# A layernorm stage in a macaron block: the first two token tiles one by one, and later statistics put behind earlier normalisations

## The chip, the cores and the metric

One Trainium2 chip, one of its cores. The metric is the device time of one execution in microseconds (us). A kernel is run several times; the median is what counts. One further execution is recorded by the hardware profiler: its profile gives every instruction's start and duration on the five engines (TensorE "PE", VectorE "DVE", ScalarE "ACT", GpSimd "POOL", SyncE "SP") and the transfers.

## The reference

The input x has 8 x 256 tokens of 256 float32 values. The block adds three terms to it:

```python
x = x + 0.5 * ffn(layernorm(x))
x = x + attention(layernorm(x))          # top-32 keys chosen by an indexer
x = x + 0.5 * ffn(layernorm(x))

def layernorm(x): return (x - mean(x)) / sqrt(var(x) + 1e-5)

def ffn(x):                               # 8 experts of width 176, 2 per token, and a shared one of 352
    scores = softmax(x @ gate_w); topk_w, topk_idx = top_k(scores, 2)
    routed = sum over the chosen experts of weight * (silu(x @ w_gate[e]) * (x @ w_up[e])) @ w_down[e]
    shared = silu(x @ sw_gate) * (x @ sw_up) @ sw_down
    return routed + shared
```

The change concerns the first line only: the layernorm ahead of the first FFN.

## The kernel before, in words

The 2,048 tokens are 16 tiles (NT) of 128 tokens, one token per partition. x stays in SBUF for the whole kernel. The kernel is written as dataflow on tiles; a scheduler at build time orders each engine's instructions and sets the waits, and that order is then fixed in the program. Each engine runs its own list strictly in order. `tc.issue_after(ins)` adds an edge that only tells this scheduler to put what is traced inside it behind `ins` on the same engine. A tile pool gives a tag a number of buffers (`bufs`): the next tile of that tag waits until the readers of the one that had its buffer are done, and a DMA that reads it is done when it has landed.

The first stage, up to the routing of the first FFN, runs like this:

- **Loads.** SP issues the loads of x by groups of tiles (L101 to L104), then sw_up (wsu_sb, L107) and sw_down (wsd_sb, L109 and L115). ScalarE's queue issues sw_gate with gate_w (wsg_sb, L105 and L106). x's groups are tiles 0-1, 2-3, 4-7, 8-11, 12-15. The transfers issued from SP and ScalarE share eight completion counters in turn, and a transfer on a counter that is in use waits on its issuing engine until the earlier one has landed.
- **Layernorm by group** (`layernorm`, L220). For each tile of the group VectorE takes statistics (bn_stats into st, L226; bn_aggr into mv, L227), then for the whole group adds epsilon (ve, L229). In the first FFN (`table=True`) ScalarE takes a square root (sd, L236) and VectorE the reciprocal (rstd, L237). In front of the square root of a group that starts at tile g0, L234 asks the scheduler to stay behind the copy of tile g0 - 3. Then for each tile VectorE writes xn = (x - mean) * rstd (L259), SP writes xn to xn_dram in HBM (L263), from where the routed experts gather tokens later, TensorE transposes its two halves into PSUM (pt, L266) and ScalarE copies them into xnT (L267). xn has five buffers (L258), pt two.
- **Expert loads.** After each group's layernorm the loop at L468 issues the next two of six expert loads on SP (L470): gate and up of the first half of the inputs, gate and up of the second, and the two halves of w_down (128-partition loads for gate and up, 88 partitions for w_down; 704 KB each). With five groups the first three issue a pair each.
- **Gate projection.** For each tile TensorE multiplies xnT with wsg_sb (pg, L476; a float32 product counts as two instructions in the profile for each of the two halves, so four a tile), ScalarE copies the eight router logits (lg, L483) and takes the Silu (sg, L485). pg has two buffers. The square root and the Silu use different activation tables, so ScalarE reloads a table whenever it changes from one to the other.
- **Shared expert, ahead of time.** The scheduler fills in the first tiles' second product with wsu_sb (pu, L493) and its product with sg (gt, L501); their transposes (ptg, L512) come behind the last pg.
- **Route.** When all 16 tiles' logits are there VectorE picks the two experts of each token (top, L291, and what follows), and the routed experts run block by block.

The second FFN and the attention use the same `layernorm` with `table=False`; the second FFN uses the same list `groups`.

Of the kernel before, what the change touches and what calls it, by code (L numbers as in the profile page):

```python
# [23 lines left out]
def macaron_kernel(  # L24
# [19 lines left out]
    nc = tc.nc  # L44

    B, S, D = x_in.shape
    NT = B * S // P
# [38 lines left out]
    x = res.tile([P, NT, D], F32, name="x")  # L86
# [11 lines left out]
    wk_sb = wts.tile([P, KD, HD], F32, name="wk_sb")  # L98
    wv_sb = wts.tile([P, KD, HD + HI], F32, name="wv_sb")

    starts = [0, 2, 4, 8, 12, NT]  # L101
    groups = [range(a, b) for a, b in zip(starts, starts[1:])]
    for g in groups:
        nc.sync.dma_start(out=x[:, g.start : g.stop, :], in_=xr[:, g.start : g.stop, :])  # L104
    nc.scalar.dma_start(out=wsg_sb[:, :, 0:HS], in_=sw_gate.rearrange("(k p) h -> p k h", p=P))  # L105
    nc.scalar.dma_start(out=wsg_sb[:, :, HS:], in_=gate_w.rearrange("(k p) e -> p k e", p=P))  # L106
# [108 lines left out]
    contents.append(lambda: nc.gpsimd.memset(inner, 1.0))  # L215
    contents.append(lambda: nc.gpsimd.memset(inner[:, :, 0:1], 0.0))

    turned_x = {}

    def layernorm(tiles, xn_dram=None, table=False):  # L220

        g0, n = tiles[0], len(tiles)
        mv = small.tile([P, n, 2], F32, tag="mv", name=f"mv_{g0}")
        for j, i in enumerate(tiles):
            st = small.tile([P, 6], F32, tag="st", name=f"st_{i}")
            nc.vector.bn_stats(st, x[:, i, :])  # L226
            nc.vector.bn_aggr(mv[:, j, :], st)  # L227
        ve = small.tile([P, n], F32, tag="ve", name=f"ve_{g0}")
        nc.vector.tensor_scalar(ve, mv[:, :, 1], EPS, None, ALU.add)  # L229
        rstd = small.tile([P, n], F32, tag="rstd", name=f"rstd_{g0}")  # L230
        if table:
            sd = small.tile([P, n], F32, tag="sd", name=f"sd_{g0}")
            with ExitStack() as order:
                if g0 - 3 in turned_x:  # L234
                    order.enter_context(tc.issue_after(turned_x[g0 - 3].ins))
                nc.scalar.activation(sd, ve, AF.Sqrt)  # L236
            nc.vector.reciprocal(rstd, sd)  # L237
        else:


            half = small.tile([P, n], I32, tag="half", name=f"half_{g0}")
            nc.vector.tensor_scalar(half, ve.bitcast(I32), 1, None, ALU.arith_shift_right)
            guess = small.tile([P, n], I32, tag="guess", name=f"guess_{g0}")
            nc.vector.tensor_tensor(
                guess, magic.to_broadcast([P, n]), half, ALU.subtract
            )
            y = guess.bitcast(F32)
            for it in range(3):
                sq = small.tile([P, n], F32, tag="sq", name=f"sq_{g0}_{it}")
                nc.vector.tensor_tensor(sq, y, y, ALU.mult)  # L250
                nc.vector.scalar_tensor_tensor(sq, sq, -0.5, ve, ALU.mult, ALU.mult)
                z = rstd
                if it < 2:
                    z = small.tile([P, n], F32, tag="z", name=f"z_{g0}_{it}")
                nc.vector.scalar_tensor_tensor(z, sq, 1.5, y, ALU.add, ALU.mult)
                y = z
        for j, i in enumerate(tiles):
            xn = small.tile([P, D], F32, tag="xn", name=f"xn_{i}", bufs=5)  # L258
            nc.vector.tensor_scalar(  # L259
                xn, x[:, i, :], mv[:, j, 0:1], rstd[:, j : j + 1], ALU.subtract, ALU.mult  # L260
            )
            if xn_dram is not None:
                nc.sync.dma_start(out=xn_dram[i * P : (i + 1) * P, 0:D], in_=xn)  # L263
            pt = psum.tile([P, KD, P], F32, tag="C", name=f"pt_{i}")
            for k in range(KD):
                nc.tensor.transpose(pt[:, k, :], xn[:, k * P : (k + 1) * P], ident)  # L266
            turned_x[i] = nc.scalar.copy(xnT[:, :, i * P : (i + 1) * P], pt)  # L267

    def route(n, lg, xn_dram, place, block, pool, keep, meanwhile, last):

# [179 lines left out]
    def ffn(n, pool, block_pool, behind):  # L450
# [14 lines left out]
        block = counted(f"block_{n}", [[1, NB], [0, NT * K]], dtype=BF16, pool=tables)  # L465
        while contents:
            contents.pop(0)()
        for tiles in groups:  # L468
            layernorm(tiles, xn_dram, table=(n == 0))
            for load in expert_loads[0:2]:  # L470
                load()
            del expert_loads[0:2]
            for i in tiles:
                pg = psum.tile([P, HS + E], F32, tag="A", name=f"pg_{n}_{i}")
                for k in range(KD):
                    nc.tensor.matmul(  # L476
                        pg,
                        xnT[:, k, i * P : (i + 1) * P],
                        wsg_sb[:, k, :],
                        start=(k == 0),  # L480
                        stop=(k == KD - 1),
                    )
                nc.scalar.copy(lg[:, i, :], pg[:, HS:])  # L483
                sg[i] = pool.tile([P, HS], F32, tag=f"sg{i}", name=f"sg_{n}_{i}", bufs=1)
                nc.scalar.activation(sg[i], pg[:, 0:HS], AF.Silu)  # L485
# [177 lines left out]
        tiles = list(range(NT))  # L663
# [361 lines left out]
    with (  # L1025
        tc.tile_pool(name="blocks0", bufs=3) as block_pool,
        tc.tile_pool(name="ffn0", bufs=3) as pool,
    ):
        results, combine, shared, left = ffn(0, pool, block_pool, behind=2)
        for i in left:  # L1030
            shared(i)

    with tc.tile_pool(name="attn", bufs=3, reuse_waits="tile") as pool:
# [5 lines left out]
        def begin(b0, b1):  # L1039

            tiles = range(b0 * TPB, b1 * TPB)
            for i in tiles:
                combine([i], results([i], small, 2))
            layernorm(tiles)
# [60 lines left out]
    with (  # L1105
        tc.tile_pool(name="blocks1", bufs=3, reuse_waits="tile") as block_pool,
        tc.tile_pool(name="ffn1", bufs=3, reuse_waits="tile") as pool,
    ):
        results, combine, shared, left = ffn(1, pool, block_pool, behind=2)

        def store(tiles):
            span = slice(tiles[0], tiles[-1] + 1)
            nc.sync.dma_start(out=outr[:, span, :], in_=x[:, span, :])


        late = left[-3:]
        with tc.tile_pool(name="late", bufs=1, reuse_waits="tile") as late_pool:
            for i in left[:-3]:
                shared(i)
            pairs = [range(i, min(i + 2, late[0])) for i in range(0, late[0], 2)]  # L1120
            ends = [range(late[0], late[2]), range(late[2], NT)]
            yg = {g: results(g, late_pool, 7) for g in pairs[:4] + ends + pairs[4:]}
            for i in late:
                shared(i, first=lambda: [combine(g, yg[g]) for g in ends if g[0] == i])
                store([i])
            for g in pairs:
                combine(g, yg[g])
                store(g)
# [48 lines left out]
```

## Time and profile before

| what | value |
|---|---|
| median of 5 runs | 998.19 us (992.74 to 1001.79) |
| profiled execution, its own time | 1001.58 us |
| its span in the profile | 999.8 us |
| busy, of the span | DVE 52%, ACT 41%, POOL 31% |
| first matmul | 9.33 us after the start of the span |
| first matmul behind the last pg (ptg, L512) | 40.50 us |
| routing starts on VectorE (top, L291) | 40.90 us |
| first gather of the routed experts (xs, L532) | 62.26 us |
| five x loads landed | 5.04, 6.29, 7.89, 9.39, 10.88 us |
| writes of xn, tiles 0 to 3, landed | 13.08, 13.46, 17.94, 18.33 us |
| writes of xn, tiles 4 to 7, landed | 22.90, 23.24, 23.63, 23.98 us |
| writes of xn, tiles 8 to 11, landed | 32.73, 33.14, 33.48, 33.86 us |

How to read it: lines of the order of time give start, duration, engine, source line, operation, output <- inputs, shapes and the number of instructions merged; in brackets the idle time ahead of them and what ended it. "SPq" rows are transfers being issued, not running. Times of landing are the events with which a transfer reports its end.

### The profile page before, as it was taken

To read this page: it belongs to the slowest core of one execution; us is meant where nothing else is said; L and a number is where in the kernel's file an instruction comes from. 1 tells how busy PE (TensorE), PEld (TensorE's weight loads), DVE (VectorE), ACT (ScalarE), POOL (GpSimd) and SP (SyncE) were. 2 spreads that over 40 slices of the span, in tenths; PEclk is the share of its full clock that TensorE was granted. 3 is DMA by queue.
4 is the path that set the end of the run, shared out by engine and by line. 5 is a ranking of instruction groups with operands and counts; after the bars stand their busy time and mean duration, and the time that the engine had idled before them with its cause. 6 is when DMAs were issued, how large, how long until landed. Compare 5 with 4: busy or idle time off the path is not lost. (4 is left out here: it accounts for less than half of the span.)

```text
span 999.8 us, 16028 instructions
## 1 busy us (share of the span) xinstructions
PE 939.4 (94%) x4412; PEld 745.1 (75%) x4412; DVE 516.6 (52%) x1986; ACT 406.7 (41%) x1299; POOL 306.2 (31%) x501
## 2 busy tenths in 40 slices
PE   6987889999999999999999999999989999789898
PEld 3665667689878888888888888888866757566665
DVE  4452223495767566566465665566565427223336
ACT  4512323234544444445435435435434432233331
POOL 2035655300042222232222223223233400656540
PEclk9997989999999999999999999999999999899999
DMA  9314542253242433343243243234244410323217
GB/s 305 86 53 123 161 141 75 80 141 100 52 138 82 145 111 108 104 124 103 91 133 115 88 140 106 101 106 126 98 133 131 162 56 6 85 87 90 84 55 257
DMA packets 124158, 111.98 MB, mean 112 GB/s; under 512 B 32326, under 2 KB 106022, under 8 KB 124070
## 3 DMA queue, kind: packets, MB, share of 16 engines
q1 hardware_dynamic: 107078, 63.30, 22.6%
q0 software_dynamic: 14272, 45.18, 13.1%
q10 hardware_dynamic: 2720, 2.47, 0.8%
q8 instruction: 38, 0.62, 0.3%
q14 instruction: 50, 0.41, 0.1%
HBM read 63.97 MB, written 46.92 MB: 111 GB/s over the span
## 5 line engine op out<-in xcount | busy, mean ns | idle before, releaser
L964 POOL TENSOR_TENSOR s<-s,rden 128x512 f32<-128x512 f32 x64 | 93.9, 1467 | 193.3 <-DVE rden L963 188.2
L954 ACT ACTIVATE s<-s,anm 128x32 f32<-128x32 f32 (+7 forms) x256 | 102.9, 404 | 53.3 <-DVE anm L950 26.3
L532 POOL DMA_INDIRECT xs<-xn_dram,token x74 | 71.5, 966 | 160.6 <-DVE choice_i L423 54.9
L1016 PE MATMUL pwo<-wo_sb,oT 128*128 128x256 f32 x512 | 117.4, 382 | 1.4 <-ACT oT L997 1.4
L1016 PEld LDWEIGHTS pwo<-wo_sb,oT 128*128 128x128 f32 x512 | 97.6, 192 | 27.1 <-issue 10.9
L697 PE MATMUL pqT<-xnT,wq_sb 128*128 128x256 f32 x512 | 116.8, 379 | 0.7 <-ACT qT L747 0.7
L555 PE MATMUL pgu<-wall,xsT 128*128 x296 | 107.1, 486 | 0.2 <-ACT xsT L545 0.2
L697 PEld LDWEIGHTS pqT<-xnT,wq_sb 128*128 128x128 f32 x512 | 96.7, 190 | 12.6 <-ACT qT L747 1.1
L697 PE MATMUL pqi<-xnT,wi_sb 128*128 128x224 f32 x512 | 103.3, 353 | 0.0
L990 PE MATMUL pav<-s,v 128*128 128x512 f32 x192 | 94.5, 596 | 2.5 <-DMA s<-sq_dram 2.5
L697 PEld LDWEIGHTS pqi<-xnT,wi_sb 128*128 128x128 f32 x512 | 95.7, 190 | 0.8
L591 PE MATMUL py<-wall,hT 88*128 x296 | 83.2, 405 | 10.7 <-DVE hT L585 6.4
L930 PE MATMUL ps<-kT,qT 128*128 128x160 f32 (+7 forms) x512 | 85.9, 310 | 4.9 <-DVE amx L939 2.4
L930 PEld LDWEIGHTS ps<-kT,qT 128*128 128x128 f32 x512 | 75.8, 191 | 19.0 <-ACT r L836 8.9
L610 POOL DMA_INDIRECT y_dram<-y,dest x74 | 72.0, 973 | 57.4 <-ACT xsT L545 29.5
L939 DVE CUSTOM_DVE_ANT_0 s<-ps,bias 128x32 f32<-128x32 f32 (+7 forms) x256 | 65.7, 299 | 46.1 <-PE ps L930 31.0
L971 DVE STREAM_TRANSPOSE sq<-s 128x512 f32<-128x512 f32 x64 | 62.4, 975 | 52.3 <-POOL s L964 52.3
L591 PEld LDWEIGHTS py<-wall,hT 88*128 88x128 f32 x296 | 59.0, 204 | 38.1 <-DVE hT L585 11.3
L821 DVE SCALAR_TENSOR_TENSOR acc<-r,iwp,acc 128x96 f32<-128x96 f32 x168 | 74.8, 498 | 11.7 <-ACT r L836 11.6
L567 DVE TENSOR_TENSOR h<-sl,pgu 128x176 f32<-128x176 f32 x74 | 25.0, 338 | 92.7 <-ACT sl L565 69.9
L997 ACT COPY oT<-pav 128x512 f32<-128x512 f32 x64 | 37.4, 584 | 71.5 <-PE pav L990 71.3
L555 PEld LDWEIGHTS pgu<-wall,xsT 128*128 128x128 f32 x296 | 53.2, 201 | 17.3 <-issue 2.2
(163 smaller groups left out, 1405.9 us busy)
## 6 DMA issues: line engine op xcount, KB each, us to landing
s<-sq_dram SPq DMA_DIRECT2D x384, 64.0 KB
sq_dram<-sq POOLq DMA_DIRECT2D x32, 512.0 KB
sq_dram<-sq POOLq DMA_DIRECT2D x32, 256.0 KB
yg<-y_dram SPq DMA_DIRECT2D x18, 256.0 KB
xn_dram<-xn SPq DMA_DIRECT2D x32, 128.0 KB
yg<-y_dram SPq DMA_DIRECT2D x7, 512.0 KB
acc_dram<-acc SPq DMA_DIRECT2D x8, 368.0 KB
wi_sb<-in_L_attn_wq_idx_dram SPq DMA_DIRECT2D x8, 256.0 KB
```

The source lines that it names most:

```text
L532: nc.gpsimd.indirect_dma_start(out=xs[b], out_offset=None, in_=xn_dram, in_offset=bass.IndirectOffsetOnAxis(ap=token[:, b : b + 1], axis=0),)
L555: nc.tensor.matmul(pgu, xsT[b][:, k, :], w[:, bass.ds(c0[b] + 2 * k * HE, 2 * HE)], start=(k == 0), stop=(k == KD - 1),)
L591: nc.tensor.matmul(py, hT[b][:, c, :], w[0:HH, bass.ds(c0[b] + 2 * KD * HE + c * D, D)], start=(c == 0), stop=(c == 1),)
L610: stored = nc.gpsimd.indirect_dma_start(out=y_dram, out_offset=bass.IndirectOffsetOnAxis(ap=dest[:, b : b + 1], axis=0), in_=y, in_offset= ...
L697: nc.tensor.matmul(ps[:, j, :], weights(k, h0 + hh + j), xnT[:, k, b * S + skip : (b + 1) * S], start=(k == 0), stop=(k == KD - 1),)
L821: nc.vector.scalar_tensor_tensor(acc[:, cols], r, iw, acc[:, cols], ALU.mult, ALU.add)
L930: nc.tensor.matmul(ps[:, c0 - first : c0 - first + n], qT[:, t * NQ + q].rearrange("p h k -> p (h k)"), kT[:, 0:n], start=True, stop=True,)
L939: nc.vector.tensor_tensor_reduce(out=s[:, q, 0:n], in0=ps[:, c0 - first : c0 - first + n], in1=bias[t][:, c0 : c0 + n], scale=1.0, scalar= ...
L954: nc.scalar.activation(scores, scores, AF.Exp, bias=nm[:, q : q + 1], scale=SCALE, accum_out=den[:, q : q + 1],)
L964: nc.gpsimd.tensor_tensor(s, s, rden.unsqueeze(2).to_broadcast([P, NQ, ns]), ALU.mult)
L990: nc.tensor.matmul(po.rearrange("p h r -> p (h r)"), v[:, c, 0:HD], pT[:, c].rearrange("p h r -> p (h r)"), start=(c == 0), stop=(c == t),)
L1016: nc.tensor.matmul(po, oT[:, h, :], wo_sb[:, w0 + h, :], start=(h == 0), stop=(h == HW - 1),)
```

## The change

The loads and the layernorm of the first FFN use six groups (0, 1, 2-3, 4-7, 8-11, 12-15); the second FFN keeps the five of before. In the first FFN, once two groups have been traced, each bn_stats is put behind the last normalisation (L259) of the group before the previous one on VectorE. The rule that holds a square root behind an earlier copy is rewritten: for g0 > 1 it stays behind the copy of tile max(g0 - 3, 0). Since two expert loads follow each group, the six of them follow tile 0, tile 1 and tiles 2-3.

```diff
-    starts = [0, 2, 4, 8, 12, NT]
-    groups = [range(a, b) for a, b in zip(starts, starts[1:])]
-    for g in groups:
+    def grouped(*starts):
+        return [range(a, b) for a, b in zip(starts, (*starts[1:], NT))]
+
+    groups = [grouped(0, 1, 2, 4, 8, 12), grouped(0, 2, 4, 8, 12)]
+    for g in groups[0]:
         nc.sync.dma_start(out=x[:, g.start : g.stop, :], in_=xr[:, g.start : g.stop, :])
...
-    turned_x = {}
+    turned_x, normalised = {}, []
...
             st = small.tile([P, 6], F32, tag="st", name=f"st_{i}")
-            nc.vector.bn_stats(st, x[:, i, :])
+            with ExitStack() as order:
+                if table and len(normalised) > 1:
+                    order.enter_context(tc.issue_after(normalised[-2].ins))
+                nc.vector.bn_stats(st, x[:, i, :])
             nc.vector.bn_aggr(mv[:, j, :], st)
...
             with ExitStack() as order:
-                if g0 - 3 in turned_x:
-                    order.enter_context(tc.issue_after(turned_x[g0 - 3].ins))
+                if g0 > 1:
+                    order.enter_context(tc.issue_after(turned_x[max(g0 - 3, 0)].ins))
                 nc.scalar.activation(sd, ve, AF.Sqrt)
...
-            nc.vector.tensor_scalar(
+            ended = nc.vector.tensor_scalar(
                 xn, x[:, i, :], mv[:, j, 0:1], rstd[:, j : j + 1], ALU.subtract, ALU.mult
             )
...
             turned_x[i] = nc.scalar.copy(xnT[:, :, i * P : (i + 1) * P], pt)
+        normalised.append(ended)
...
-        for tiles in groups:
+        for tiles in groups[n]:
             layernorm(tiles, xn_dram, table=(n == 0))
             for load in expert_loads[0:2]:
                 load()
             del expert_loads[0:2]
```

In the built program the order of the instructions differs from before only in this first stage: 2 instructions more on VectorE, 1 on ScalarE and 1 on SP, TensorE's the same in number, GpSimd's the same in order.

## The prediction

> **What bounds the kernel now.** I read the page first, for the share of each engine, then the order of time of the first 41 us on TensorE, on VectorE and on the SP queue, then the transfers of that stretch. The change touches only the first FFN's layernorm, so the question is what sets the end of that stage and whether the rest waits for it.
>
> ```profile
> span 999.8 us, 16028 instructions
> PE 939.4 (94%) x4412; PEld 745.1 (75%) x4412; DVE 516.6 (52%) x1986; ACT 406.7 (41%) x1299; POOL 306.2 (31%) x501
> ```
>
> TensorE is the bound of the whole. A microsecond matters if TensorE's stream moves by it.
>
> ```profile
> 9.33 1.09 PE L266 MATMUL pt<-ident,xn 128*128 128x128 f32 x4 [9.33 <-DVE xn L259]
> 10.45 5.17 PE L476 MATMUL pg<-wsg_sb,xnT 128*128 128x360 f32 x8
> ...
> 17.11 2.58 PE L476 MATMUL pg<-wsg_sb,xnT 128*128 128x360 f32 x8
> ...
> 36.26 4.40 PE L476 MATMUL pg<-wsg_sb,xnT 128*128 128x360 f32 x14
> 40.50 0.71 PE L512 MATMUL ptg<-ident,gt 128*128 128x128 f32 x5
> ```
>
> TensorE starts at 9.33, and from there to 40.50 one group follows the next without a gap. The same eight pg matmuls take 5.17 us at first and 2.58 later: about 0.60 against 0.302 us each, half speed until about 15.4. After that 14 tiles need 56 pg x 0.302 + 28 transposes x 0.109 + 16 pu x 0.296 = 24.7 of the 25.1 us to the end: the stage is TensorE-bound.
>
> ```profile
> 7.91 0.75 DVE L226 BATCH_NORM_STATS2 st<-x 128x6 f32<-128x256 f32 x2 [0.36 <-DMA x<-in_L_attn_x_dram]
> 8.58 0.21 DVE L237 RECIPROCAL rstd<-sd 128x2 f32<-128x2 f32 x2
> ...
> 8.79 1.36 DVE L259 TENSOR_SCALAR xn<-x,mv,rstd 128x256 f32<-128x256 f32 x4
> ...
> 17.96 0.41 DVE L259 TENSOR_SCALAR xn<-x,mv,rstd 128x256 f32<-128x256 f32 x1
> ...
> 22.57 0.84 DVE L259 TENSOR_SCALAR xn<-x,mv,rstd 128x256 f32<-128x256 f32 x2
> ...
> 32.75 1.24 DVE L259 TENSOR_SCALAR xn<-x,mv,rstd 128x256 f32<-128x256 f32 x3 [1.92 <-DMA xn_dram<-xn]
> ```
>
> The first reciprocals (8.58) stand in VectorE's order behind statistics of tiles 4 and 5, whose load landed at 7.89, though their square roots were done at 7.15 and 7.79. The last row is the other thing to see: normalising tile 13 waited for a write to xn_dram. xn has five buffers, so tile i waits until the write of tile i-5 has landed. Tile 7 (17.96) and tile 9 (second of the 22.57 row) start within 0.1 us of such landings too (17.94 and 22.90).
>
> ```profile
> 19.76 1.44 SPq L121 DMA_DIRECT2D wall<-in_L_ffn_w_down_dram  x2
> 23.01 11.48 SPq L263 DMA_DIRECT2D xn_dram<-xn  x8
> ```
>
> ```profile
> GB/s 0 35 190 378 346 352 347 348 360 381 374 357 359 351 333 351 304 329 368 380 290 187 221 204 208 162 170 186 276 65 220 129 0 15 0 0 0 0 0 0
> ```
>
> Slices of 1.125 us from 0 to 45. The queue runs at 330 to 380 GB/s from 3.4 to 22, then at about 160 to 220 from 24 to 31: that is the two w_down loads. The write of tile 8 was issued at 23.01 behind them and landed at 32.73. What SP issues later lands later, so the order on SP sets when xn buffers come free.
>
> **The change, part by part.**
>
> (1) Tiles 0 and 1 loaded alone: one more x load, one more SP issue (0.45 to 0.5 us each). The loads carry the same bytes in the same order, so tile 1 lands about when the pair did (5.04; I take 5.1) and everything later as before. wsu and what follows now waits for a landing first and is issued near 5.5 instead of 3.74, still well before the loads ahead of it end at 10.88: nothing.
>
> (2) Statistics, root and reciprocal per tile: one more each of ve, sd, reciprocal (0.26, 0.20, 0.15 us rows). Tile 0's own landing buys nothing, since in VectorE's new order its ve stands behind tile 1's statistics. But the two reciprocals now stand ahead of all later statistics. From 5.1: bn 0.34, ag and ve 0.4, root 0.2, reciprocal and hand-overs 0.35 give the first xn at 6.4 (before 8.79), the first transpose at 6.9 (9.33), the first pg at 8.0 (10.45). TensorE starts 2.4 us sooner. The root of tiles 2 and 3 stands ahead of tile 1's copy on ScalarE and holds it to 9.0; pg of tile 0 runs to 10.4 at half speed, so that is hidden.
>
> (3) Statistics put behind the last normalisation but one: the bn and ag rows of tiles 8 to 15 (0.33 and 0.09 us of issue each) leave the 11 to 15.5 stretch and go between normalisations from 11 to 23. VectorE was idle 17.9 to 22.3 and 23.4 to 24.5; no cost.
>
> (4) What moves with it on SP. Two expert loads are issued after every group. With groups of 1, 1, 2, 4 in place of 2, 2, 4 the order becomes: write 0, gate and up, write 1, gate and up, writes 2 and 3, **the two w_down loads, and only then writes 4 to 7**. Before, writes 4 to 7 stood ahead of w_down. From before's landings: a gate/up pair 4.05 us (13.46 to 17.50), a write 0.35 to 0.45, the w_down pair with one write behind it 8.75 (23.98 to 32.73). So write 0 lands at 13.1, write 1 at 13.1 + 4.05 + 0.4 = 17.5, write 2 at 22.0, write 3 at 22.4, **write 4 at 22.4 + 8.75 = 31.2** (before 22.90), writes 5 to 7 at 31.5 to 32.3. Tile 9 can thus be normalised at 31.2 instead of 22.9.
>
> TensorE until then: eight pg at half speed from 8.0 to 12.8; tiles 2 to 8 are 28 pg x 0.302 + 14 transposes x 0.109 + 16 pu x 0.296 = 14.7, and about 1.3 us lost at tile 7, whose buffer comes at 22.0: it has nothing left at 28.8 to 29.1. It waits until 31.2 + 0.4 (xn) + 0.1 = 31.7. Seven tiles remain: 7 x (0.22 + 1.21) = 10.0, so 41.7. With the backlog gone, ScalarE's order shows: the copy of tile 9 before its pg 0.4; the square-root table load (1.28) ahead of the copies of 10 and 11, 0.3; the Silu table load (1.28) ahead of the sg that frees pg's bank for tile 11, 0.5. That makes 42.9 where before had 40.7. **Sum: +2.2 us.** The 2.4 us won at the start are spent waiting at 29.
>
> After it the route stage waits for the last lg (VectorE idle 6.9 us before top at 40.90), and from there both programs have the same order on every engine: the shift passes on whole.
>
> Unknown: the clock after the wait. TensorE would stand 2.6 us. From below: no drop, 0. From above: the granted clock was 0.95 from 40.7 to 62.3 though TensorE was 21.3 of 21.6 us busy, so a thin stretch is enough for about 2.2 us at half speed; a drop of 3 to 4 us here costs 1.7, and 10.0 us of work wholly at half speed would cost 5. I take 0, as the nearest row (the 0.95 stage) lost about 1 us for far longer thin work, and keep 5 for the range.
>
> The skill has a rule on this: the Trainium skill, "TensorE: Matmul & The Clock Gate", "What's actually happening", says that the array falls back to half rate after an idle window of about 3.4 us and needs a busy one to recover. The half-speed row at 10.45 agrees with the slow start; by the rule a wait of 2.6 us is too short and the sum stays at +2.2, a wait over 3.4 us would make it about +3.9.
>
> A second one speaks on w_down: "DMA: Bandwidth & Descriptors", "Why a DMA increments its semaphore by 16 and not by 1", says a transfer uses the largest number of engines up to 16 that divides its partitions, so 11 for these 88. My estimate from it at 350 GB/s x 11/16 is 6.0 us for 1,408 KB; write 4 would land at 28.8 and the sum would be about 0. The measured 8.75 decides.
>
> **Against the runs.** The profiled execution took 1001.58 us (span 999.8), 3.4 above the median of the five runs, 998.19. 1001.58 + 2.2 stands to 998.19 + 2.2 = 1000.4. I predict 1000.5 us. Under about 1% this kernel's times can't be told from no change.
>
> **Rivals.**
>
> A. The early start survives and it ends faster. Place: landing of write 4; price: if w_down moved like gate and up (1,408 KB in 4.05 us), write 4 lands at 22.4 + 4.4 = 26.8, TensorE never stands at 29, and the stage ends between 40.3 (tile 7's wait and the three ScalarE waits stay) and 39.2 (they go): -0.4 to -1.5, 996.7 to 997.8. It decides if write 4 lands before about 28.5. For it: five engines' share of the queue is free meanwhile. Against: 23.98 to 32.73 is the same pair in the same place. Chance 0.17.
>
> B. The wait comes and the clock drops with it: +2.2 + 1.7 to 5, 1002.1 to 1005.4. For: the 0.95 stage. Against: 2.6 us is short. Chance 0.2.
>
> C. Slower by over 1%: w_down is much slower behind the new order. It decides from write 4 landing at 39, that is 16.6 us for what took 8.75; each microsecond more is one microsecond at the end. Its slowest slice before (162 GB/s) gives 8.9 us for the pair, so nothing read here reaches it. Chance 0.07, for that and for what the trace does not show.
>
> D. No effect at all: the stage would have to be hidden behind something. VectorE's 6.9 us idle before top says it isn't. Chance 0.03.
>
> **How the numbers follow.** My forecast 0.53 (+1 to +3, 999 to 1001.5), A 0.17, B 0.2, C 0.07, D 0.03. All but C and a remainder lie within 1% of 998.19 (988.2 to 1008.2). The runs of before alone span 992.74 to 1001.79, so a median may lie 3 us off; -1.5 - 3 and +5.5 + 3.5 about 998.2 make 994 to 1007. Faster by over 1%: 0.03, within: 0.89, slower: 0.08.
>
> **What would show it.** Right: first transpose near 7 and first pg near 8; xn of tile 9 at about 31 waiting for a write to xn_dram; TensorE idle 2 to 3 us just before tile 9's transposes; the first ptg matmul near 42.7; the stretch behind it as long as before. Wrong: if tile 9 is normalised before 28, (4) is wrong and A holds; if pg rows after 31.7 take 0.6 us each, B holds; if the first transpose stays near 9, (2) is wrong; if the first ptg and the end move by different amounts, the shift does not pass on.

## The result, and the profile after

The kernel after took 1002.9 us (median of 52 runs, 995.46 to 1011.34), the kernel before 997.5 us in 94 runs beside it (990.49 to 1007.42). The ratio is 1.0052, 95% interval 1.0040 to 1.0063: slower by about 5.2 us (4.0 to 6.3). 1000.5 us, or +2.2, was predicted. The direction and the place were right, the size was too small. The profiled execution of after took 1001.33 us.

The page of after, the same two lines as of before: TensorE has the same number of matmuls and is as full as it was.

```profile
span 999.6 us, 16029 instructions
PE 934.4 (93%) x4412; PEld 741.8 (74%) x4412; DVE 517.0 (52%) x1988; ACT 407.1 (41%) x1300; POOL 306.2 (31%) x501
```

The two spans (999.6 and 999.8) say nothing about the change. Single executions of one kernel lie up to 17 us apart, so the change is read in the first 45 us and in the medians. The order of time on TensorE (source lines are those of the kernel after: its L264, L268, L271 and L482 are L259, L263, L266 and L476 of before):

```profile
6.45 1.09 PE L271 MATMUL pt<-ident,xn 128*128 128x128 f32 x4 [6.45 <-DVE xn L264]
7.57 4.58 PE L482 MATMUL pg<-wsg_sb,xnT 128*128 128x360 f32 x8
...
17.80 0.41 PE L271 MATMUL pt<-ident,xn 128*128 128x128 f32 x2 [0.58 <-DVE xn L264]
...
22.36 0.41 PE L271 MATMUL pt<-ident,xn 128*128 128x128 f32 x2 [1.14 <-DVE xn L264]
...
28.24 0.76 PE L499 MATMUL pu<-wsu_sb,xnT 128*128 128x352 f32 x2
31.38 1.13 PE L271 MATMUL pt<-ident,xn 128*128 128x128 f32 x4 [2.39 <-DVE xn L264]
32.31 1.55 PE L482 MATMUL pg<-wsg_sb,xnT 128*128 128x360 f32 x2
...
37.48 1.48 PE L482 MATMUL pg<-wsg_sb,xnT 128*128 128x360 f32 x4 [0.37 <-ACT sg L491]
...
44.08 0.82 PE L518 MATMUL ptg<-ident,gt 128*128 128x128 f32 x6
```

The start is 2.88 us sooner (6.45 for 9.33), and the end of the stage 3.58 us later (44.08 for 40.50). Between them stand three waits for xn in brackets, where before had none: 0.58 (tile 6), 1.14 (tile 7) and 2.39 us (tile 9, from 28.99 on). A fourth, 0.37 us, is for a Silu on ScalarE. The first eight pg, at half speed, took 4.58 us here and 5.17 in before's profile; this length comes back below. Behind the last, two pg matmuls take 1.55 us; later in the stage 16 take 5.01.

VectorE's order of time names what tile 9 waited for:

```profile
5.37 0.16 DVE L242 RECIPROCAL rstd<-sd 128x1 f32<-128x1 f32 x1
5.72 0.16 DVE L242 RECIPROCAL rstd<-sd 128x1 f32<-128x1 f32 x1 [0.19 <-ACT sd L241]
...
21.81 0.41 DVE L264 TENSOR_SCALAR xn<-x,mv,rstd 128x256 f32<-128x256 f32 x1 [2.78 <-DMA xn_dram<-xn]
...
30.91 1.17 DVE L264 TENSOR_SCALAR xn<-x,mv,rstd 128x256 f32<-128x256 f32 x3 [6.15 <-DMA xn_dram<-xn]
```

The reciprocals are at 5.37 and 5.72 (8.58 before). The three tiles 9 to 11 at 30.91 wait 6.15 us for a write of xn: write 4 landed at 30.89, writes 5 to 7 at 31.29, 31.65 and 32.02. Before, write 4 landed at 22.90. The SP queue's rows give the reason, the w_down pair issued ahead of the last twelve writes:

```profile
14.91 2.66 SPq L268 DMA_DIRECT2D xn_dram<-xn  x2
17.62 2.20 SPq L123 DMA_DIRECT2D wall<-in_L_ffn_w_down_dram  x2
19.92 16.36 SPq L268 DMA_DIRECT2D xn_dram<-xn  x12
```

The completion events of write 4 in the trace say the same more closely: five of its sixteen came at 23.63 to 23.71, the other eleven only at 29.70 to 30.89, after the eleven of the second w_down load at 29.36 to 30.51. (Each w_down load has eleven such events, besides one at its issue; a gate or up load has sixteen.) So part of the write was through early, and the rest stood behind w_down.

The last view is the table of stretches. Its columns are the stretch, its length, busy time (and instructions) on PE, PEld, DVE, ACT and POOL, then granted clock, DMA share and GB/s.

```profile
25.00:28.50 3.50, 3.50 (x14) 2.26 (x13) 0.00 (x0) 1.00 (x5) 0.00 (x0) 1.00 0.79 194
28.50:31.90 3.40, 0.96 (x5) 0.26 (x3) 0.98 (x3) 0.51 (x3) 0.00 (x0) 1.00 0.59 164
31.90:35.30 3.40, 3.40 (x9) 2.07 (x10) 1.60 (x6) 2.46 (x5) 0.00 (x0) 0.50 0.35 118
35.30:38.70 3.40, 3.03 (x13) 1.90 (x12) 0.14 (x1) 2.88 (x7) 0.00 (x0) 1.00 0.46 154
```

The stretches are cut where the clock record changes. In the second TensorE works 0.96 of 3.40 us; in the third it is granted half its clock, just when tiles 9 to 11 have arrived and it has work. The prediction had taken this at nothing.

### The profile page after: what moved, and what is told of

The parts are those of the page before. It is cut to its first block, busy times and chain, and to the rows that moved or that the text cites. A ratio compares the mean times of both kernels' runs of the same rounds, so it can differ in the third digit from the quotient of the medians.

```text
span 999.6 us, 16029 instructions
## 1 busy us (share of the span) xinstructions
PE 934.4 (93%) x4412; PEld 741.8 (74%) x4412; DVE 517.0 (52%) x1988; ACT 407.1 (41%) x1300; POOL 306.2 (31%) x501
## 4 chain that ended last, share of the span: by engine, by line
PE 41%; DMA 7%; DVE 6%; issue 5%; SPq 4%; ACT 4%; POOL 2%; another core or an unknown queue 0%; ACTq 0%; DVEq 0%; POOLq 0%
PE pwo L1022 7%; PE pqT L703 6%; PE pqi L703 5%; PE ps L936 4%; PE pav L996 4%; PE py L597 3%; ACT s L960 3%; PE pgu L561 3%; SPq L988 3%; DMA sq_dram<-sq 2%; DMA y_dram<-y,dest 2%; POOL s L970 2%; PE pi L834 2%; PE pg L482 2%; PE po L525 1%
## 5 line engine op out<-in xcount | busy, mean ns | idle before, releaser
L561 PE MATMUL pgu<-wall,xsT 128*128 x296 | 104.0, 474 | 0.2 <-ACT xsT L551 0.2
```

Of the source, the lines that this page charges most:

```text
L561: nc.tensor.matmul(pgu, xsT[b][:, k, :], w[:, bass.ds(c0[b] + 2 * k * HE, 2 * HE)], start=(k == 0), stop=(k == KD - 1),)
```

## The experiments

Theory Q, the queue: the early w_down pair makes write 4 land late, write 4 holds the buffer of tile 9, and TensorE runs dry. Rivals: V, that the new order on VectorE and ScalarE costs the time; N, that the loss isn't in this stage. Later a theory K on the clock. "First ptg" is the start of the first matmul behind the last pg, the end of the stage. Not every build has the same work ahead of it: before, after, e2, e3, e4, e7 and e11 have 16 pu matmuls there, e1, e6 and e12 have 14, and e8 to e10 have 8, at 0.296 us each. The experiments' runs came from three chips. Each ratio is the one on record against runs of before on the same chip, and needn't be the quotient of the two medians.

**e1: twelve xn buffers.**

```diff
-            xn = small.tile([P, D], F32, tag="xn", name=f"xn_{i}", bufs=5)
+            xn = (own or small).tile([P, D], F32, tag="xn", name=f"xn_{i}", bufs=12 if own else 5)
...
-            layernorm(tiles, xn_dram, table=(n == 0))
+            layernorm(tiles, xn_dram, table=(n == 0), own=tables if n == 0 else None)
```

> The changed kernel with 12 xn buffers in the first FFN instead of 5; SP's order stays as changed, w_down ahead of writes 4 to 7. Queue theory (the loss is tile 9's wait for the buffer that the write of tile 4 holds until it lands behind w_down, near 31 us): the wait goes though write 4 still lands near 31; TensorE runs without a gap from its start near 6.5, the first ptg matmul is at 37 to 38.5 us (before 40.5, changed 44.1), no stretch at half clock near 32, and the time is 2 to 3.5 us below before, ratio 0.9965 to 0.998. Rival 1 (the loss comes from the new order on VectorE and ScalarE): nothing changes, first ptg near 44, ratio about 1.005. Rival 2 (the loss is not in this stage at all): first ptg moves to about 38 but the time stays about 1.003 to 1.005.

Measured: 949.55 us against 952.31, ratio 0.9973 (0.9958 to 0.9987). First transpose 6.45, first ptg 37.16. The table of stretches and the order of time on TensorE of this kernel:

```profile
16.00:46.00 30.00, 29.88 (x129) 20.23 (x128) 12.08 (x48) 19.23 (x55) 0.00 (x0) 1.00 0.60 163
```

```profile
37.16 0.82 PE L520 MATMUL ptg<-ident,gt 128*128 128x128 f32 x6
```

TensorE is busy 29.88 of 30 us, the clock is whole, and the stage ends 6.9 us before after's, 0.6 of it because two pu matmuls stand behind the first ptg. Write 4 still landed late, at 31.56. Groups, statistics and the order of the transfers are those of after; the buffers no longer wait for the writes, and the scheduler then orders TensorE and ScalarE a little differently. That is Q, and the version is faster than before here, and than after in e12.

**e2: the queue's order of before.**

```diff
-            for load in expert_loads[0:2]:
-                load()
-            del expert_loads[0:2]
+            if tiles[0] > 0 or n > 0:
+                for load in expert_loads[0:2]:
+                    load()
+                del expert_loads[0:2]
```

> The changed kernel, but no expert loads behind tile 0's group, so that SP's order of writes and expert loads is that of before (writes 0 and 1, gate and up, writes 2 and 3, gate and up, writes 4 to 7, w_down). Queue theory: write 4 lands near 23 again, TensorE does not stand at tile 9, first ptg at 38 to 39.5 us, 1 to 2.5 us below before, ratio 0.9975 to 0.999. Rival 1 (VectorE and ScalarE order): first ptg stays near 44, ratio 1.005. Rival 2: first ptg near 39, ratio still 1.003 or more.

Measured: 950.86 us, ratio 0.9986 (0.9971 to 1.0001). First transpose 6.45, first ptg 39.12. Its SP queue, then its TensorE:

```profile
15.36 3.79 SPq L268 DMA_DIRECT2D xn_dram<-xn  x4
19.20 1.98 SPq L123 DMA_DIRECT2D wall<-in_L_ffn_w_down_dram  x2
21.28 13.25 SPq L268 DMA_DIRECT2D xn_dram<-xn  x8
```

```profile
33.27 0.95 PE L271 MATMUL pt<-ident,xn 128*128 128x128 f32 x4 [0.98 <-DVE xn L264]
...
39.12 0.82 PE L519 MATMUL ptg<-ident,gt 128*128 128x128 f32 x6
```

Four writes stand ahead of w_down again. The early start survives, and two waits are left: 0.78 us for tile 7 at 18.07, and 0.98 us for tile 13, whose buffer write 8 held until 32.77. VectorE and ScalarE do all that they do in after; V would have kept the loss.

**e3: before, with w_down moved ahead of writes 4 to 7** (and with it the second gate and up pair ahead of writes 2 and 3), and nothing else.

```diff
-            for load in expert_loads[0:2]:
+            take = 4 if tiles[0] == 0 else 2
+            for load in expert_loads[0:take]:
                 load()
-            del expert_loads[0:2]
+            del expert_loads[0:take]
```

> The kernel before with its five groups, but both gate and up pairs issued behind the first group and w_down behind the second: w_down then stands ahead of writes 4 to 7, and nothing else of the change is made. Queue theory: write 4 lands near 31, tile 9 is normalised near 31 instead of 22.9, TensorE stands about 1 us there, ScalarE's table loads show, first ptg at 42 to 44.5 us, ratio 1.002 to 1.005. Rival 1 (VectorE and ScalarE order): first ptg stays at 40.5, ratio 1.000. Rival 2: ratio 1.000 with first ptg moved.

Measured: 956.08 us, ratio 1.0047 (1.0032 to 1.0062). First ptg 43.49, and no half clock before 62.7. Tile 9's transposes wait again:

```profile
32.12 0.89 PE L266 MATMUL pt<-ident,xn 128*128 128x128 f32 x4 [1.16 <-DVE xn L259]
```

The loads alone, with not one statistic moved, make the kernel before as slow as after.

**e4: after, without the edge that puts statistics behind normalisations.**

```diff
-                if table and len(normalised) > 1:
+                if False:
```

> The changed kernel without the edge that puts statistics behind the last normalisation but one. Queue theory: SP's order is the same as in the changed kernel, so tile 9 still waits until about 31 and the first ptg stays at 43 to 44.5, ratio 1.004 to 1.006; the first transpose may start later, up to 9. Rival 1 (the order of the statistics costs the time): first ptg back at 40.5 or less, ratio about 1.000.

Measured: 956.76 us, ratio 1.0044 (1.0026 to 1.0062). First transpose 7.86, first ptg 44.48, and the wait ahead of tile 9:

```profile
31.77 0.91 PE L271 MATMUL pt<-ident,xn 128*128 128x128 f32 x4 [2.49 <-DVE xn L264]
```

The edge brings the first transpose forward by 1.4 us; it isn't what costs, since the loss stays without it.

**e11: before, with that edge and nothing else.**

```diff
-            nc.vector.bn_stats(st, x[:, i, :])
+            with ExitStack() as order:
+                if table and len(normalised) > 1:
+                    order.enter_context(tc.issue_after(normalised[-2].ins))
+                nc.vector.bn_stats(st, x[:, i, :])
```

> The kernel before with one part of the change alone: the statistics of a group are issued behind the normalisation of the last group but one; groups and loads stay 2, 2, 4, 4, 4, so the queue's order is that of the kernel before (write 4 to 7 ahead of the w_down pair). The queue theory: this is the part that gains. The first reciprocals no longer stand behind the statistics of tiles 4 and 5, so TensorE starts between 6.9 and 8 (before 9.33), writes land as before (write 4 near 22 to 23), there is no wait at tile 9, and the first ptg is at 39.0 to 40.0 (before 40.50), ratio 0.998 to 1.000. Rival, that the moved statistics are what costs (they stand between the normalisations): first ptg later than 40.5, ratio over 1.002.

Measured: 1007.46 us against 1005.49, ratio 1.0008 (0.9982 to 1.0035). First transpose 8.47, 0.5 us later than the latest expected, no gap, first ptg 39.18. That is 1.3 us ahead of before's profile, but only 0.86 of it is the start (8.47 for 9.33); the rest is that the first eight pg took 4.63 us for 5.17, which other profiles do without the edge (4.75 in e3, 4.62 in e6). The interval is too wide to show that in the time, but the rival's ratio of over 1.002 isn't excluded by the time either, only its later ptg by the trace.

**e6: before, with twelve buffers** (the edit of e1 on the kernel before).

> The kernel before with twelve xn buffers in place of five in the first FFN, nothing else. The queue theory: before has TensorE without a gap from 9.33 to 40.50, so its buffers cost it nothing, the wait at tile 13 goes and nothing moves: first ptg 40.2 to 40.5, ratio 0.999 to 1.001. Rival, that the gain of the version with twelve buffers and the change came from the buffers alone: first ptg near 37 to 38, ratio near 0.997.

Measured: 1005.74 us, ratio 1.0006 (0.9973 to 1.0039). First ptg 39.51, 0.7 us below what was expected: this run's first transpose came at 8.99 (9.33), its first eight pg took 4.62 us (5.17), and it has two pu matmuls fewer ahead of the first ptg. No wait for xn, as in before. It is far from the 37 to 38 us of the rival, whose ratio near 0.997 the interval just reaches: buffers without the early start bring little, since TensorE had no wait for them.

**e7: w_down in loads of 80 and 8 partitions.**

```diff
...
-            wall[0:HH, :, c0 : c0 + D],
-            w_down[:, c * HH : (c + 1) * HH, :].rearrange("e h d -> h e d"),
+            for a, z in ((0, 80), (80, HH)):
+                nc.sync.dma_start(
+                    out=wall[a:z, :, c0 : c0 + D],
+                    in_=w_down[:, c * HH + a : c * HH + z, :].rearrange("e h d -> h e d"),
+                )
...
```

> The kernel after, with each w_down load (88 partitions) cut into one of 80 and one of 8 partitions; nothing else is changed, and the number of bytes and the place in the queue stay. The queue theory says that write 4 lands late only because the w_down pair ahead of it moves slowly (8.75 us for 1,408 KB in the trace of before, where gate and up take 4.05). If the slowness comes from the partitions, as the Trainium skill has it in "DMA: Bandwidth & Descriptors", "Why a DMA increments its semaphore by 16 and not by 1", the pair moves faster: write 4 lands near 27, tile 9 is normalised before TensorE runs out at 28.8, the 2.4 us wait is gone, no half clock near 32, first ptg at 39 to 41 in place of 44.08, ratio to before 0.997 to 1.000. Rival: the slowness has another cause (the rows of w_down lie far apart, or all loads of this stretch share a limit): write 4 lands at 30 to 32 as in the kernel after, wait and half clock stay, ratio 1.004 to 1.006.

Measured: 1006.51 us against 1005.55, ratio 0.9992 (0.9962 to 1.0022). Write 4 landed at 29.06, 6.39 us behind write 3, for 8.71 in after; from tile 8's normalisation to tile 9's it is 6.0 us (23.08 to 29.09) for 8.4 (22.47 to 30.91). TensorE's wait shrinks to 0.54 us, now for tile 10 at 30.54; there is no half clock near 32, and the first ptg is 41.09, at the upper end of what was expected. Two stretches of after, a gate and up pair and then the w_down pair, and the w_down pair in e7:

```profile
13.20:15.20 2.00, 2.00 (x8) 1.23 (x8) 1.55 (x7) 0.25 (x3) 0.00 (x0) 1.00 1.13 361
...
26.20:28.20 2.00, 2.00 (x8) 1.27 (x7) 0.00 (x0) 0.42 (x2) 0.00 (x0) 1.00 0.76 181
```

```profile
25.00:27.00 2.00, 2.00 (x9) 1.31 (x8) 0.34 (x3) 1.10 (x5) 0.00 (x0) 1.00 1.09 237
27.00:29.00 2.00, 2.00 (x8) 1.29 (x7) 0.00 (x0) 0.23 (x1) 0.00 (x0) 1.00 0.93 302
```

Read the last two columns. With 88 partitions the DMA share is 0.76 at 181 GB/s (0.74 to 0.93 at 181 to 233 in the pair's four stretches of 2 us), where gate and up have 1.13 at 361. In e7 it is 1.09 again, but at 237 GB/s, and at the pair's end 0.93 at 302. Both theories hold in part. In after it is 8.71 us from the landing of write 3 to that of write 4, with w_down between, and 4.56 from write 1 (17.22) to write 2 (21.78), with gate and up between. Of these 4.15 us the split takes back 2.3. The rest goes with a lower rate at a full DMA share, whose cause wasn't tried.

**e8, e9, e10: the wait filled.** Theory K: the half clock follows from the wait and costs the rest. In all three kernels tile 8's pg stands behind tile 11's transposes and pu of tiles 2 and 3 behind tile 15's pg, so that TensorE has nothing of its own during the wait, and N added matmuls with an unread result run there: one of 8 columns, five of 360, nine of 360. The order on TensorE is otherwise the same in the three.

```diff
...
+            if table and i == 8:
+                spin = psum.tile([P, HS + E], F32, tag="D", name="spin")
+                with tc.issue_after(turned.ins):
+                    for _ in range(N):
+                        filler.append(nc.tensor.matmul(spin, xnT[:, 0, 6 * P : 7 * P],
+                                                       wsg_sb[:, 0, :], start=True, stop=True))
...
```

> First of three kernels with one order of instructions on TensorE, VectorE, the queue and GpSimd, which differ in the work put on TensorE between tile 8's transposes and tile 9's. All are the kernel after with tile 8's shared gate matmuls held behind tile 11's transposes and the shared up matmuls of tiles 2 and 3 behind tile 15's gate matmuls, so that nothing of its own is left for TensorE while tile 9 is waited for; one added matmul of 8 columns, whose result nobody reads. TensorE should stand from about 26 to 31.4, 5.4 us. Every theory of the clock says that it falls here: half rate for 3 to 4 us after 31.4, first ptg near 45.5, some 1.7 us behind the kernel with the wait filled.

> Second of the three: in the same place five added matmuls of 360 columns (2 instructions of 0.302 us each, 3.0 us in all), so TensorE stands about 2.5 us before tile 9's transposes, as long as in the kernel after. If the clock falls after any thin stretch of this length (what the 31.91 to 35.33 at half clock in the kernel after suggest), the half rate and its 1.4 to 1.7 us are here too, and the first ptg is near that of the kernel with one small matmul. Rival, the rule of the Trainium skill, "TensorE: Matmul & The Clock Gate", "What's actually happening", that an idle window of about 3.4 us is needed: no fall here, first ptg as in the kernel with nine.

> Third of the three: nine added matmuls of 360 columns (5.4 us in all), so TensorE works until about 31.3 and has no wait before tile 9's transposes; tile 9 is normalised as late as in the kernel after. Theory: the rest of the kernel after's loss (beyond the wait itself) is the clock; full clock throughout, first ptg near 43.8, 1.4 to 1.7 us before the kernel with one small matmul, and the time 1 to 2 us lower than that kernel's. Rival: the half clock near 32 has nothing to do with the wait (it comes at that age of the program whatever TensorE did): the same half-rate stretch here and no difference among the three.

| kernel | ratio to before (interval) | TensorE's wait ahead of tile 9, us | half clock, 25 us to first ptg | first ptg |
|---|---|---|---|---|
| e8, one small | 1.0055 (1.0025 to 1.0086) | 5.99 | 6.8 us | 45.41 |
| e9, five | 1.0033 (1.0004 to 1.0062) | 2.73 | none | 44.35 |
| e10, nine | 1.0046 (1.0013 to 1.0080) | none | none | 44.11 |

Between e8 and e10 tile 9's transposes differ by 0.09 us, the ends by 1.30 (1.4 to 1.7 was expected): so the half clock costs about 1.3 us of this stage. The times are too close to tell the three apart. That e9 has no half clock was the surprise, as its wait (2.73 us) is longer than after's (2.39). The stretches, cut again at the steps of the clock record, of e8, then of e9, then one of e10:

```profile
25.95:29.37 3.42, 0.00 (x0) 0.00 (x0) 0.00 (x0) 0.00 (x0) 0.00 (x0) 1.00 0.75 165
29.37:32.78 3.41, 1.37 (x6) 0.91 (x7) 1.17 (x3) 0.69 (x2) 0.00 (x0) 0.50 0.55 178
32.78:36.20 3.42, 3.42 (x8) 2.11 (x8) 1.56 (x5) 2.27 (x6) 0.00 (x0) 0.50 0.33 111
```

```profile
27.30:30.70 3.40, 1.76 (x6) 0.76 (x4) 0.00 (x0) 0.00 (x0) 0.00 (x0) 1.00 0.74 190
30.70:34.10 3.40, 2.24 (x10) 1.44 (x11) 1.18 (x3) 1.83 (x4) 0.00 (x0) 1.00 0.48 161
```

```profile
30.40:33.80 3.40, 3.31 (x15) 1.87 (x14) 1.17 (x3) 1.88 (x3) 0.00 (x0) 1.00 0.47 155
```

The clock goes in steps of 3.4 us whose phase differs from run to run. In after one step held the whole wait (0.96 us busy); in e9 the wait fell across two (1.76 and 2.24 busy) and the clock stayed.

**The kernel after once more**, to try that reading:

> The kernel after, unchanged, once more, for the phase of the clock: its wait before tile 9 should be 2.3 to 2.7 us again and the first ptg between 42.7 and 44.4. If the half clock after the wait depends on how the wait lies to the clock's steps of about 3.4 us (it was there when most of one step was idle, not when the wait was split over two), it is here only if one step of the clock record holds more than about 2 us of the wait; then the first ptg is near 44, else near 43. Ratio to before 1.003 to 1.007.

Measured: 1011.53 us against 1005.49, ratio 1.0053 (1.0022 to 1.0084). The wait ahead of tile 9 is 2.13 us (2.3 to 2.7 was expected), the first ptg 43.91, and the clock:

```profile
28.10:31.50 3.40, 1.27 (x6) 0.56 (x4) 0.65 (x2) 0.53 (x2) 0.00 (x0) 1.00 0.54 159
31.50:34.90 3.40, 3.40 (x10) 1.95 (x10) 1.47 (x6) 2.49 (x5) 0.00 (x0) 0.50 0.36 120
```

One step held the whole wait (3.40 - 1.27 = 2.13 us), and the half clock followed. e4 agrees (0.88 us busy from 29.1 to 32.5, half from 32.5). In this stage a step with 0.88, 0.96 or 1.27 us of matmuls was followed by half clock, one with 1.76 or 2.24 was not. The whole clock records say how far that goes. Over all steps of the fourteen profiles, each of the 53 at full clock with less than 1.45 us of matmuls was followed by half clock; of 49 with 1.45 to 1.92 us 28 were; of 3,741 with more, nine, all in full work at 53 to 60 us of nine profiles. So after's wait belongs where the clock always fell, while e9's 1.76 us lies where it could have gone either way: that its clock stayed doesn't show the reading by itself. How often an execution of after has its wait across two steps wasn't counted; its two profiles and e4's, with a like wait, all show the half clock.

**The version with twelve buffers once more, beside after on the same chip:**

> The kernel after with twelve xn buffers in the first FFN, the version that beat both, once more, beside the kernel after on the same chip. Queue theory: first ptg near 37.2, no TensorE gap at tile 9, no half clock before 45 from it, ratio to before 0.996 to 0.999 and 6 to 8 us below the kernel after. Rival, chance on the first chip: ratio 0.999 or more.

Measured: 1004.23 us, ratio 0.9968 (0.9943 to 0.9993), 7.3 us below after's 1011.53. First ptg 37.88, no gap, no half clock before 57.5. By the ratio the gain of e1 is there on a second chip; the medians alone would make it smaller (1004.23 for 1005.49).

## Why the prediction was right in direction and short in size

**Step 1, single loads: nothing.** Right: SP's first write is issued at 6.33, and nothing is later for the added load. sw_up was issued at 4.15, where 5.5 was expected.

**Step 2, TensorE starts 2.4 us sooner.** Right: 2.88 us (first transpose 6.45 for a predicted 6.9, first pg 7.57 for 8.0). The difference is that tile 1's load, taken at 5.1, had landed when VectorE began its statistics at 4.62. e4 and e11 share the 2.88 out: the single tiles without the edge bring 1.47 (start 7.86), the edge without them 0.86 (8.47), so neither brings most of it alone.

**Step 3, moved statistics: no cost.** Right, by e2 (moved statistics, no loss) and e4 (free statistics, the same loss).

**Step 4, the queue.** Right to 0.3 us at each place. Write 4 landed at 30.89 (31.2 predicted), TensorE was empty at 28.99 (28.8 to 29.1) and went on at 31.38 (31.7). The wait at tile 7 was 1.14 us (1.3). One of 0.58 us at tile 6 wasn't in the sum; the earlier start paid for it. e1, e2 and e3 take this cause away or bring it alone, and the loss goes and comes with it. Rival A is out, as the pair took as long behind the new order as before.

**The failed step is "Unknown: the clock after the wait. ... I take 0".** From the transposes at 31.38 to the first ptg it took 12.70 us for a predicted 11.0. e9 and e10, without half clock, take 12.56 and 12.64 with one tile's pg more behind the wait (eight tiles for seven, 4 x 0.302 = 1.21), so 11.35 and 11.43. The half clock is the other 1.3, which is also the difference between e8 and e10, though over unlike stretches: e8's matmuls behind the wait were slow for longer and took 2.1 us more than e10's, and a wait of 0.54 us for ScalarE that e10 has was hidden by that. The two bounds of the prediction held (0 and 5 us); the value was taken at the wrong end, by a row and with a rule that would have said the same. The row, the stretch with 0.95, wasn't one of thin work: its half step (from 59.93 us on) follows a step in which TensorE worked all 3.41 us, so it can't price a wait. The Trainium skill, "TensorE: Matmul & The Clock Gate", "What's actually happening", speaks of an idle window of about 3.4 us, free-running. The steps of 3.4 us with a phase of their own are in these rows; but the window needn't be idle: 1.27 us of work in it didn't keep the clock. So rival B, at 0.2, came true beside the forecast, at a little under its lower price of 1.7, and 1002.9 lies in its range (1002.1 to 1005.4), not in the forecast's own (999 to 1001.5). The time came as near to 1000.5 as it did partly by luck: the five runs it was counted from had a median 0.7 us above that of the 94.

With this the stage adds up: +2.2 predicted, -0.3 (write 4 earlier), +1.3 (clock), +0.35 (the tiles behind the wait): 3.55 for the 3.58 measured at the first ptg, and 3.58 too at the first gather (65.84 for 62.26). The 1.3 and the 0.35 come out of the same 12.70 us, so that the sum closes is no proof of them; the 1.3 stands on e8 and e10.

**"The shift passes on whole".** Open in size. The times say 5.2 (4.0 to 6.3), the stage 3.6, and 3.4 in the second profile. Some half a microsecond of the difference may be before's one profile: its first eight pg took 5.17 us, where the three others that start at 8.47 to 9.60 (e3, e6, e11) have 4.62 to 4.75. Before had no wait until 40.50, so with their length it would end near 40.0, while after's end follows write 4; that makes the stage about 4.1, an estimate from these rows. The remaining 1.1 to 1.6 couldn't be placed: behind the route stage the clock record falls to half for 27 to 56 us in all, at places that differ from run to run (42.2 us in before's profile, 29.0 in after's), and that hides a microsecond. On the chip of e1 to e4 the records held 5 to 8 us of it, and there the four ratios follow the stage: first ptg at 37.16, 39.12, 43.49 and 44.48, that is -3.3 (-2.7 with the two pu matmuls counted), -1.4, +3.0 and +4.0 us against the 40.50 of before's profile, with -2.6, -1.3, +4.5 and +4.2 by the ratios. Theory N is out as the main cause; whether a part of what remains is another wait or half steps set off by the shift isn't settled.

## What to carry to other kernels

When a load is moved forward in a queue, list what now stands behind it there, and whose buffers those transfers give back. Here 1,408 KB of weights that nobody needed yet held a 128 KB write, and the write held a buffer that fed the bounding engine. An early start is worth having only with the buffers to run ahead: in the order of transfers of after, five buffers turned it into a loss (1.005) and twelve into a gain (0.997), and twelve without the early start changed nothing that could be measured (1.0006). And a wait on TensorE can cost more than its length: here 1.3 us more, when it left less than 1.45 us of matmuls in one 3.4 us step of the clock record.

## What the runs showed of the hardware, beyond what was expected

- The granted clock changes in steps of 3.4 us with a phase that differs from run to run. In the fourteen profiles half clock followed every step in which TensorE worked less than 1.45 us, 28 of 49 with 1.45 to 1.92 us, and of the others only nine, full of work, at 53 to 60 us, for which no cause was looked for. e8 stayed at half through a step with 1.37 us and was whole again after one full of work; e4 and e11 each stayed at half through a full one (at 63.2 and 57.9 us).
- A load over 88 partitions kept the DMA share at 0.74 to 0.93, the same data in 80 and 8 partitions brought it to 1.09 and was 2.3 us quicker for 1,408 KB. Even so its rate was 237 to 302 GB/s for 361 of a 128-partition load. The Trainium skill, "DMA: Bandwidth & Descriptors", "Why a DMA increments its semaphore by 16 and not by 1", has the rule for the number of engines, which gives 11 for 88 partitions and 16 for 80; the eleven completion events of each w_down load and the shares agree with it. The rate per engine is a second term, and the estimate of 6.0 us for the pair, made from that page without it, stands against 8.71 measured (a 128 KB write included).
- The kernel before took 952.31 us on one chip and 1005.5 on two others, at a mean granted clock of 0.997 and 0.978 to 0.979. On one chip an execution is about 10 us longer per 0.01 of clock, which makes 18 or 19 of the 53 us; the others show in no column read here.
